# A macaron block's setup in one written order: loads, FFN weight, first tiles and the split of the other weights

## The chip, the cores and the metric

The kernel runs on one core of one Trainium2 chip. The metric is device time in microseconds (us), the median of three runs of the kernel before. Smaller is better.

## The reference

The input `x` has 4 x 4096 rows of 512 numbers. The block is: half an FFN, neighbourhood attention, half an FFN, each on a layer-normed input, with a residual.

```python
x = x + 0.5 * ffn(layernorm(x), weight, ffn_bias)
x = x + attention(layernorm(x), qkv_w, qkv_b, rpb, proj_w, proj_b)
x = x + 0.5 * ffn(layernorm(x), weight, ffn_bias)
```

The "FFN" is one 512 x 512 linear layer, `xd @ wd.T + bias`. Both its operands are first quantised in blocks of 32 along the row: the scale of a block is its largest magnitude over 7.5, the quotients are rounded to a grid of 6-bit floats, and multiplied by the scale again. The attention has 16 heads of 32; each of the 4096 rows of a sequence attends to 13 neighbours, with a relative bias table `rpb` of 16 x 25, and its output goes through the projection `proj_w`.

## The kernel before

**Tiles and products.** The 16384 rows are 128 tiles `t` of 128 rows. Four tiles are a group, and an attention item `m` is one group with one of four chunks of heads. Every 512-wide product is done in float16 with both operands split into a high and a low part: `product` (L139) issues 12 matmuls of 128 x 512. The weights lie transposed in one tile `wt` (L122), 20 chunks `o` of 128 output rows: 0 to 3 query, 4 to 7 key, 8 to 11 value, 12 to 15 projection, 16 to 19 FFN.

**The slots.** After the setup the order is a list of slots written out by hand. `begin(slot, stage)` puts a generator into a slot, `run_slot` runs its next part, and a part yields how many slots later its next one runs. One item takes `STEP` = 7 slots. A tile goes through `quantised_norms` (L213: factors on POOL, normalise on ACT, block maxima `sc` and reciprocals `r` on DVE, quotients `yq` on POOL, rounding `q` on ACT, scaling back `yq` on POOL, high part `hlq` on ACT, low part `hlq` on DVE, transposition to `xT` by a DMA from SP), `first_half` (L274: FFN product `pmf`, residual, statistics, normalise `yn`, high and low part `hln`, transposition into the group's tile `x2`), `values` (L296: product `pmv`, high and low part `vt`, a store of it to DRAM), and, from slot `QK` = 38 on, `project_qk` (L354: product `pmqk`, high part `qf` on ACT, low part on DVE), `softmax`, `attend`, `project_out` and `second_half`.

**The head.** It is what stands before slot `QK` (L673 to L891). It loads the FFN weight `fw`, three biases, the relative bias `rp`, the first tiles, and the 16 chunks `rows` of the other weights. Each weight matrix is scaled by a power of two, which `powers` (L716) makes from the largest sum of squares of a chunk: squares on ACT, a maximum `top` on DVE, a transposition `ptn` and a small product `pb` on TensorE, and eight small steps on DVE that give `up` and `down`. The FFN weight is quantised (L760 to L784), then split into high and low part and transposed by DMAs from SP. `put_scaled` (L795) does the split of the other chunks, through four buffers `whl`: ACT writes the high part, DVE the low part, and SP transposes it into `wt`. `attention_bias` (L827) adds the value bias's projection to `after_b`; `put_table` (L874) makes the table of relative biases from `shifted` (eight loads from the DRAM tile `rd`) and `masks` (four).

**What sets the order.** Up to L793 a scheduler in the language's library orders the instructions of each engine by its own estimate; from `tc.manual_schedule()` on they stand as the code issues them. Every engine then works through its own instructions in that order, and so does each queue of DMA issues: nearly all of them stand on SP, the loads of the two broadcast biases (L681, L682), of `b12` and of `rp` on ACT. A DMA from SP also waits until the DMA eight before it on the same set of semaphores has landed. The pools of the head are released at its end, and tiles of the attention reuse their memory.

Of the kernel before, what the change touches and what calls it, by code (L numbers as in the profile page):

```python
# [37 lines left out]
P = 128  # L38
# [25 lines left out]
def macaron_kernel(  # L64
# [148 lines left out]
    def quantised_norms(slot):  # L213
# [7 lines left out]
        if spare:  # L221
            y = xp.tile([P, dim], F32, tag="x", name=f"yq{slot}").unsqueeze(1)
        else:
            y = yp.tile([P, 2, dim], F32, tag="yq", bufs=2, name=f"yq{slot}")[:, :n]
# [16 lines left out]
        q8 = q8p.tile([P, 2, dim], F8, tag="q8", name=f"q8_{slot}")[:, :n]  # L241
# [6 lines left out]
        if spare:  # L248
# [355 lines left out]
    EARLY = 3  # L604
# [35 lines left out]

    for t in range(NT):
        k = t * STEP
        sooner = (0, 2, 5, STEP)[t] if t <= EARLY else 0
        begin(k - 18 - (STEP if t == EARLY else 0), one(load, t), 0)
        slot = k - 10 - (10 if t == EARLY else 0)
        enlist(slot, t, "n1")
        if not 0 < t < EARLY:
            begin(slot - 1, one(moments, slot, t, "n1"), 1)
        begin(k + F1 - sooner, first_half(t))
        begin(k + V, values(t))  # L650
        begin(k + F1 - sooner, one(add_bias, t, half_ffn_b), 8)
# [6 lines left out]
    for slot in together:  # L658
        if together[slot][0][0][1] == "n3" or together[slot][0][0][0] >= EARLY:
            begin(slot, quantised_norms(slot), 1)  # L660
# [11 lines left out]

    with tc.tile_pool(name="setup", bufs=1) as sp, tc.tile_pool(name="scratch", bufs=2) as scr:  # L673
# [4 lines left out]
        rp = sp.tile([HEADS, NREL + 2 * (QR - 1)], F32, name="rp")  # L678
        for o in range(KC):
            nc.sync.dma_start(out=fw[:, o, :], in_=ffn_w[o * P : (o + 1) * P, :])  # L680
        nc.scalar.dma_start(out=half_ffn_b, in_=ffn_b.partition_broadcast(P))  # L681
        nc.scalar.dma_start(out=after_b, in_=proj_b.partition_broadcast(P))  # L682
        nc.scalar.dma_start(out=b12, in_=qkv_b.rearrange("(c p) -> c p", p=P))
        nc.gpsimd.memset(rp, 0.0)
        nc.scalar.dma_start(out=rp[:, QR - 1 : QR - 1 + NREL], in_=rpb)


        rows = {}

        sq = sp.tile([P, 5 * KC], F32, name="sq")  # L690
        first = min(slots)
        for slot in range(first, first + EARLY * STEP, STEP):
            run_slot(slot)
        for _ in quantised_norms(-10):
            pass
        chunks = (8, 9, 10, 11, 12, 13, 14, 15, 0, 4, 1, 5, 2, 6, 3, 7)
        for o in chunks:
            w, i = (qkv_w, o) if o < 3 * KC else (proj_w, o - 3 * KC)
            rows[o] = xp.tile([P, dim], F32, tag="x", name=f"rows{o}")
            nc.sync.dma_start(out=rows[o], in_=w[i * P : (i + 1) * P, :])  # L700
        for o in (*range(4 * KC, 5 * KC), *chunks):
            src = fw[:, o - 4 * KC, :] if o >= 4 * KC else rows[o]
            junk = scr.tile([P, dim], BF16, tag="junk", name=f"junk{o}")
            nc.scalar.activation(junk, src, AF.Square, accum_out=sq[:, o : o + 1])
        ptb = ps_m.tile([P, 512], F32, tag="mm", name="ptb")
        nc.tensor.transpose(ptb[:, : 3 * KC], b12, ident[: 3 * KC, : 3 * KC])
        bT = sp.tile([P, 3 * KC], F32, name="bT")
        nc.vector.tensor_copy(bT, ptb[:, : 3 * KC])
        b2 = sp.tile([P, 3 * KC], F32, name="b2")
        nc.vector.scalar_tensor_tensor(b2, bT, 2.0 ** -8, bT, ALU.mult, ALU.mult)  # L710
        nc.vector.tensor_tensor(sq[:, : 3 * KC], sq[:, : 3 * KC], b2, ALU.add)
        top5 = sp.tile([P, 5], F32, name="top5")
        up = sp.tile([P, 5], F32, name="up")
        down = sp.tile([P, 5], F32, name="down")

        def powers(lo, hi):  # L716

            w = hi - lo
            nc.vector.tensor_reduce(
                top5[:, lo:hi], sq[:, lo * KC : hi * KC].rearrange("p (m c) -> p m c", c=KC),  # L720
                AX.X, ALU.max,
            )
            ptn = ps_m.tile([P, 512], F32, tag="mm", name=f"ptn{lo}")
            nc.tensor.transpose(ptn[:w, :P], top5[:, lo:hi], ident)
            most = sp.tile([w, 1], F32, name=f"most{lo}")
            nc.vector.tensor_reduce(most, ptn[:w, :P], AX.X, ALU.max)
            diag = sp.tile([w, w], F32, name=f"diag{lo}")
            nc.vector.tensor_scalar(diag, ident[:w, :w], most, 2.0, ALU.mult, ALU.mult)
            ones_w = sp.tile([w, P], F32, name=f"ones{lo}")
            nc.gpsimd.memset(ones_w, 1.0)  # L730
            pb = ps_m.tile([P, 512], F32, tag="mm", name=f"pb{lo}")
            nc.tensor.matmul(pb[:, :w], ones_w, diag, start=True, stop=True)
# [16 lines left out]
        def put_weights(o, hl):  # L749
# [3 lines left out]
            )  # L753

        w_sc, w_r, w_back = (
            sp.tile([P, KC * NB], F32, name=name) for name in ("w_sc", "w_r", "w_back")
        )
# [178 lines left out]
```

## Time and profile before

| | us |
|---|---|
| median of 3 runs (2294.38 to 2295.41) | 2294.65 |
| the profiled execution | 2295.28 |
| its span | 2293.5 |
| PE busy in the span | 2214.2 (97%) |
| DVE busy | 2011.7 (88%) |
| POOL busy | 1969.2 (86%) |
| ACT busy | 1695.5 (74%) |

PE is TensorE's matmuls, PEld its weight loads, DVE VectorE, ACT ScalarE, POOL GpSimd, SP SyncE; SPq is the queue of SP. A row of the timeline has the start in us from the span's start, the duration, the engine, the line, the operation, output and inputs, the shapes, the number of instructions merged into the row, and in brackets how long the engine had been idle and what it had waited for. The chain of waits is the work that ended last, followed back from the end, as start, duration and what it is. The time of any one run agrees with another of the same kernel within 0.05% here.

### The profile page before, as it was taken

What the parts mean: (1) busy time and instruction counts of PE and PEld (TensorE: products, weight loads), DVE (VectorE), ACT (ScalarE), POOL (GpSimd) and SP (SyncE); (2) the same over time, 40 slices, a digit from 0 to 9 for tenths busy, and PEclk for the clock granted to TensorE, in tenths of its full rate; (3) what the DMA queues carried; (4) which work ended last, traced back from release to release, by engine and by line L of the source; (5) the groups of instructions that cost most, each with busy time, mean ns of one, the idle gap of its engine ahead of it and who ended that gap; (6) DMA issues with size and microseconds to landing.
All of it is one profiled execution on the core that took longest, in us unless ns stands there. A gap on an engine that the chain in (4) does not pass through costs nothing.

```text
span 2293.5 us, 65425 instructions
## 1 busy us (share of the span) xinstructions
PE 2214.2 (97%) x26771; PEld 1052.9 (46%) x26771; DVE 2011.7 (88%) x3769; ACT 1695.5 (74%) x2544; POOL 1969.2 (86%) x2006
## 2 busy tenths in 40 slices
PE   3799999999999999999999999999999999999978
PEld 1344444444444444444444444444444444444433
DVE  6899998888988988898988998888988988989775
ACT  5697777777777777777777777777777777777752
POOL 4588988988988988888888888888888889888776
PEclk9999999999999999999999999999999999999989
DMA  7687776777767777777776776777776777866654
GB/s 201 153 178 161 162 160 154 159 162 158 160 156 155 164 162 154 161 158 157 162 158 155 162 161 154 160 157 155 164 160 151 167 158 154 166 155 147 137 107 104
DMA packets 926213, 359.61 MB, mean 157 GB/s; under 512 B 719452, under 2 KB 890328, under 8 KB 925912
## 3 DMA queue, kind: packets, MB, share of 16 engines
q1 hardware_dynamic: 925568, 354.90, 70.8%
q8 instruction: 209, 3.42, 0.6%
q14 instruction: 92, 0.75, 0.1%
q10 hardware_dynamic: 344, 0.53, 0.1%
HBM read 110.26 MB, written 67.29 MB: 77 GB/s over the span
## 4 chain that ended last, share of the span: by engine, by line
PE 87%; DVE 7%; ACT 2%; POOL 2%; DMA 1%; issue 1%; SPq 0%; ACTq 0%; DVEq 0%; POOLq 0%
PE pmqk L144 27%; PE pmf L144 26%; PE pmo L144 14%; PE pmv L144 13%; PE ps L458 4%; PE pv L549 3%; DVE stn L173 1%; DVE hlq L197 1%; DVE hln L197 1%; DVE sc L232 1%; ACT qk L390 0%; DVE x L272 0%; POOL yq L239 0%; DVE total L514 0%; DVE qf L383 0%
## 5 line engine op out<-in xcount | busy, mean ns | idle before, releaser
L144 PE MATMUL pmf<-wt,xT 128*128 128x512 f16 x3048 | 702.7, 381 | 13.3 <-DMA xT<-hlq 7.4
L144 PE MATMUL pmqk<-x,wt 128*128 128x512 f16 x3072 | 705.8, 379 | 0.4 <-DVE after_b L836 0.4
L144 PEld LDWEIGHTS <-xT 128*128 128x128 f16 x3048 | 298.4, 98 | 377.2 <-DMA xT<-hlq 15.2
L144 PEld LDWEIGHTS <-wt 128*128 128x128 f16 x3072 | 289.7, 98 | 336.0 <-issue 1.3
L239 POOL TENSOR_TENSOR yq<-yq,r 128x1024 f32<-128x1024 f32 (+1 forms) x141 | 247.1, 1752 | 135.6 <-DVE r L237 124.1
L144 PE MATMUL pmv<-wt,x 128*128 128x512 f16 x1536 | 353.9, 380 | 4.2 <-DVE qf L383 2.6
L144 PE MATMUL pmo<-wt,ring 128*128 128x512 f16 x1536 | 357.2, 383 | 0.0
L390 ACT ACTIVATE qk<-qf,parity 128x1024 f16<-128x1024 f16 x256 | 349.3, 1432 | 0.0
L610 POOL TENSOR_TENSOR x<-x,half_ffn_b 128x512 f32<-128x512 f32 x256 | 327.8, 1281 | 0.0
L272 DVE SCALAR_TENSOR_TENSOR x<-pmf,coef,x 128x512 f32<-128x512 f32 x256 | 180.0, 703 | 144.7 <-PE pmf L144 141.1
L576 ACT ACTIVATE ring<-pv 128x510 f16<-128x510 f32 (+7 forms) x176 | 78.7, 475 | 307.3 <-PE pv L549 234.4
L173 DVE BATCH_NORM_STATS2 stn<-x 128x6 f32<-128x512 f32 x384 | 265.2, 691 | 8.8 <-DMA x<-in_L_attn_x_dram 0.2
L244 POOL TENSOR_TENSOR yq<-q,sc 128x1024 f32<-128x1024 fp8e4 (+1 forms) x141 | 246.2, 1746 | 4.8 <-ACT q L242 4.8
L144 PEld LDWEIGHTS <-x 128*128 128x128 f16 x1536 | 150.5, 98 | 186.9 <-issue 4.9
L242 ACT ACTIVATE q<-yq,nudge 128x1024 fp8e4<-128x1024 f32 (+1 forms) x141 | 150.0, 1064 | 115.9 <-POOL yq L239 107.6
L144 PEld LDWEIGHTS <-ring 128*128 128x128 f16 x1536 | 141.2, 98 | 160.5 <-issue 5.0
L518 POOL TENSOR_TENSOR sf<-sf,total 128x714 f32<-128x714 f32 (+2 forms) x128 | 178.7, 1396 | 37.2 <-DVE total L516 19.3
L226 ACT ACTIVATE yq<-x,nbq,rsq 128x512 f32<-128x512 f32 x254 | 193.1, 803 | 16.7 <-POOL nbq L185 15.2
L525 POOL TENSOR_TENSOR p<-sf,p 128x714 f16<-128x714 f32 (+2 forms) x128 | 192.5, 1504 | 0.0
L509 POOL TENSOR_TENSOR sf<-sf,top 128x714 f32<-128x714 f32 (+2 forms) x128 | 182.4, 1425 | 3.5 <-DVE top L507 3.3
L197 DVE TENSOR_TENSOR hlq<-yq,hlq 128x1024 f16<-128x1024 f32 (+1 forms) x141 | 167.6, 1189 | 8.7 <-ACT hlq L193 6.6
L610 POOL TENSOR_TENSOR x<-x,after_b 128x512 f32<-128x512 f32 x128 | 162.9, 1274 | 0.0
(143 smaller groups left out, 3441.0 us busy)
## 6 DMA issues: line engine op xcount, KB each, us to landing
vs<-vd SPq DMA_DIRECT2D x144, 357.0 KB
x<-in_L_attn_x_dram SPq DMA_DIRECT2D x128, 256.0 KB
vd<-vt SPq DMA_DIRECT2D x128, 256.0 KB
out_dram<-x SPq DMA_DIRECT2D x128, 256.0 KB
vs<-vd SPq DMA_DIRECT2D x24, 378.0 KB
vs<-vd SPq DMA_DIRECT2D x24, 315.0 KB
rows<-in_L_attn_qkv_w_dram SPq DMA_DIRECT2D x12, 256.0 KB
xT<-hlq SPq DMA_TRANSPOSE x141
```

Of the source, the lines that this page charges most:

```text
L144: nc.tensor.matmul(pm, lhs(a, c), rhs(b, c), start=(n == 0), stop=(n == 3 * KC - 1))
L173: nc.vector.bn_stats(st, xs[t])
L197: nc.vector.tensor_tensor(hl[:, :, 1, :], y, hl[:, :, 0, :], ALU.subtract)
L226: nc.scalar.activation(y[:, u], xs[t], AF.Identity, bias=nb[:, u : u + 1], scale=rs[:, u : u + 1])
L239: nc.gpsimd.tensor_tensor(yb, yb, bc(r, QB), ALU.mult)
L244: nc.gpsimd.tensor_tensor(yb, q8.rearrange("p u (n q) -> p (u n) q", q=QB), bc(sc, QB), ALU.mult)
L272: nc.vector.scalar_tensor_tensor(xs[t], pm, cf, xs[t], ALU.mult, ALU.add)
L390: nc.scalar.activation(to, whole[0], AF.Copy, scale=parity[:, e : e + 1])
L509: nc.gpsimd.tensor_tensor(s, s, bc(top[:, :n], KN), ALU.subtract)
L518: nc.gpsimd.tensor_tensor(s, s, bc(total[:, :n], KN), ALU.mult)
L525: nc.gpsimd.tensor_tensor(p[:, :n, KN : 2 * KN], s, ph, ALU.subtract)
L610: nc.gpsimd.tensor_tensor(xs[t], xs[t], b, ALU.add)
```

## The change

The head is no longer ordered by the library's scheduler. `tc.manual_schedule()` is called ahead of it, every step becomes a small function, and each is entered in a list with a key. The list is sorted by the keys and run in that order; a key decides nothing but the place. What is computed is the same, but for the places where the arithmetic moves: the FFN weight's scale is applied in the split (`split`, as for the other chunks) and no longer in the factor `w_back`.

- Loads: `fw` in four pieces first, then `x` tiles 0 and 1, then the FFN bias row, then the query, key and value chunks with `x` tiles 2 to 4 between them. The four projection chunks, `x` tiles 5 and 6, the projection's bias row, `rp`, `masks` and `rd` come behind the FFN weight's transpositions. All but `b12` are issued by SP.
- The first seven tiles are normalised with buffers of their own (`own`), one tile at a time; `first_half` of tiles 0 to 4 and `values` of tiles 0 and 1 are in the list too. `values` of tile 2 and the product for the value bias are put into slots behind `QK`.
- The order of the chunks is 8 to 11, then query and key in pairs, and the projection's last.
- Two blocks of 12 matmuls into a tile that nobody reads (`idle`) follow the splits of the first and the last FFN chunk.

```diff
-    def quantised_norms(slot):
+    def quantised_norms(slot, own=None):
...
+        if own:
+            y = own.tile([P, 1, dim], F32, name=f"yq{slot}")
+        elif spare:
...
+        if own:
+            q8 = own.tile([P, 1, dim], F8, name=f"q8_{slot}")
+        else:
+            q8 = q8p.tile([P, 2, dim], F8, tag="q8", name=f"q8_{slot}")[:, :n]
...
+        if own:
+            hl = own.tile([P, 1, 2, dim], F16, name=f"hlq{slot}")
...
+    HEAD = 7
     for t in range(NT):
         k = t * STEP
-        sooner = (0, 2, 5, STEP)[t] if t <= EARLY else 0
-        begin(k - 18 - (STEP if t == EARLY else 0), one(load, t), 0)
-        slot = k - 10 - (10 if t == EARLY else 0)
-        enlist(slot, t, "n1")
-        if not 0 < t < EARLY:
+        if t >= HEAD:
+            if t > HEAD + 1:
+                begin(k - 18, one(load, t), 0)
+            slot = k - 10
+            enlist(slot, t, "n1")
             begin(slot - 1, one(moments, slot, t, "n1"), 1)
-        begin(k + F1 - sooner, first_half(t))
-        begin(k + V, values(t))
-        begin(k + F1 - sooner, one(add_bias, t, half_ffn_b), 8)
+        if k + F1 >= QK:
+            begin(k + F1, first_half(t))
+            begin(k + F1, one(add_bias, t, half_ffn_b), 8)
+        if k + V >= QK:
+            begin(k + V, values(t))
...
+    ctx.enter_context(tc.manual_schedule())
+    vbx = {}
     with tc.tile_pool(name="setup", bufs=1) as sp, tc.tile_pool(name="scratch", bufs=2) as scr:
...
-        for o in range(KC):
-            nc.sync.dma_start(out=fw[:, o, :], in_=ffn_w[o * P : (o + 1) * P, :])
-        nc.scalar.dma_start(out=half_ffn_b, in_=ffn_b.partition_broadcast(P))
-        nc.scalar.dma_start(out=after_b, in_=proj_b.partition_broadcast(P))
-        nc.scalar.dma_start(out=b12, in_=qkv_b.rearrange("(c p) -> c p", p=P))
...
+        ones = sp.tile([4, P], F32, name="ones")
+        nc.gpsimd.memset(ones, 1.0)
...
-        for slot in range(first, first + EARLY * STEP, STEP):
-            run_slot(slot)
-        for _ in quantised_norms(-10):
-            pass
...
+        def load_ffn(o):
+            rows[4 * KC + o] = fw[:, o, :]
+            nc.sync.dma_start(out=fw[:, o, :], in_=ffn_w[o * P : (o + 1) * P, :])
...
-        w_sc, w_r, w_back = (
-            sp.tile([P, KC * NB], F32, name=name) for name in ("w_sc", "w_r", "w_back")
-        )
...
-        nc.vector.tensor_scalar(w_back, w_sc, up[:, 4:5], None, ALU.mult)
-        for o in range(KC):
-            w8 = scr.tile([P, dim], F8, tag="w8_", bufs=KC, name=f"w8_{o}")
-            nc.scalar.activation(w8, fw[:, o, :], AF.Identity, bias=w_nudge, saturate=False)
-            nc.vector.tensor_tensor(blocks(fw[:, o, :]), blocks(w8), per(w_back, o), ALU.mult)
-            hl = scr.tile([P, 2, dim], F16, tag="whl", bufs=4, name=f"whlf{o}")
-            nc.scalar.copy(hl[:, 0, :], fw[:, o, :])
-            nc.vector.tensor_tensor(hl[:, 1, :], fw[:, o, :], hl[:, 0, :], ALU.subtract)
-            put_weights(4 * KC + o, hl)
-
...
+        def rounded(o):
+            w8[o] = scr.tile([P, dim], F8, tag="w8_", bufs=KC, name=f"w8_{o}")
+            nc.scalar.activation(w8[o], fw[:, o, :], AF.Identity, bias=w_nudge, saturate=False)
+
+        def scaled_back(o):
+            nc.vector.tensor_tensor(blocks(fw[:, o, :]), blocks(w8[o]), per(w_sc, o), ALU.mult)
+
+        def split(o):
             s = up[:, o // KC : o // KC + 1]
             hl = scr.tile([P, 2, dim], F16, tag="whl", bufs=4, name=f"whl{o}")
             nc.scalar.activation(hl[:, 0, :], rows[o], AF.Copy, scale=s)
-            yield 1, 9
+            yield
             nc.vector.scalar_tensor_tensor(
                 hl[:, 1, :], rows[o], s, hl[:, 0, :], ALU.mult, ALU.subtract
             )
-            put_weights(o, hl)
-
-        su, sd = up, down
+            nc.sync.dma_start_transpose(
+                out=wt.rearrange("p s c o -> p (s c) o")[:, :, o * P : (o + 1) * P],
+                in_=hl.rearrange("p s k -> p (s k)"),
+            )
+            if o in (4 * KC, 5 * KC - 1):
+                idle = ps_s.tile([P, 512], F32, tag="s", name=f"idle{o}")
+                for _ in range(12):
+                    nc.tensor.matmul(idle, hl[:, 1, :P], hl[:, 1, :], start=True, stop=True)
+
...
-        def attention_bias():
-
-            vbx = sp.tile([P, 2, KC, P], F16, name="vbx")
-            nc.scalar.copy(vbx[:, 0], bc(vb, P))
-            nc.vector.tensor_tensor(vbx[:, 1], bc(vb, P), vbx[:, 0], ALU.subtract)
-            yield 11, 9
-            pmb = ps_m.tile([P, dim], F32, tag="mm", name="pmb")
-            product(pmb, lambda s, c: vbx[:, s, c, :], lambda s, c: wt[:, s, c, PO : PO + dim])
-            yield 1, 9
-            nc.vector.scalar_tensor_tensor(after_b, pmb, cp, after_b, ALU.mult, ALU.add)
...
-        begin(0, one(scales), 9)
-        for slot, o in zip((2, 4, 5, 6, 10, 13, 16, 19, 21, 23, 25, 27, 29, 31, 33, 35), chunks):
-            begin(slot, put_scaled(o), 9)
-        begin(20, attention_bias(), 9)
-        begin(26, one(put_table), 9)
-        slot = first
-        while slot < QK:
-            run_slot(slot)
-            slot += 1
-
+        def attention_bias():
+            t = xp.tile([P, dim], F32, tag="x", name="vbx").bitcast(F16)
+            vbx[0] = t = t.rearrange("p (s c q) -> p s c q", s=2, c=KC)
+            nc.scalar.copy(t[:, 0], bc(vb, P))
+            yield
+            nc.vector.tensor_tensor(t[:, 1], bc(vb, P), t[:, 0], ALU.subtract)
+
+        order = []
+
+        def at(key, f, *args):
+            order.append((key, len(order), f, args))
+
+        def spread_out(gen, *keys):
+            for key in keys:
+                at(key, next, gen, None)
+
+        CHUNKS = (8, 9, 10, 11, 0, 4, 1, 5, 2, 6, 3, 7, 12, 13, 14, 15)
+        for o, key in enumerate((0.71, 1.13, 1.56, 1.99)):
+            at(key, load_ffn, o)
+        for t, key in enumerate((2.42, 2.87, 5.09, 7.07, 10.37, 26.1, 26.6) + (55.92, 61.92)):
+            at(key, load, t)
+        for o, key in zip(CHUNKS, (3.77, 4.43, 5.75, 6.41, 7.73, 8.39, 9.05, 9.71, 11.03, 11.69, 12.35, 13.01, 24.1, 24.6, 25.1, 25.6)):
+            at(key, load_row, o)
+        at(0.8, lambda: nc.scalar.dma_start(out=b12, in_=qkv_b.rearrange("(c p) -> c p", p=P)))
+        at(3.32, lambda: nc.sync.dma_start(out=half_ffn_b, in_=ffn_b.partition_broadcast(P)))
+        at(27.1, lambda: nc.sync.dma_start(out=after_b, in_=proj_b.partition_broadcast(P)))
+        at(27.6, lambda: nc.sync.dma_start(out=rp[:, QR - 1 : QR - 1 + NREL], in_=rpb))
+        at(5.97, lambda: nc.gpsimd.tensor_scalar(half_ffn_b, half_ffn_b, 0.5, None, ALU.mult))
+        for h, key in enumerate((28.1, 28.66, 29.22, 29.78)):
+            at(key, put_masks, h)
+        at(30.34, put_shifts)
+        for i, key in enumerate((32.34, 32.94, 33.54, 35.44, 36.04, 39.24, 39.84, 40.44)):
+            at(key, put_shifted, i // 4 * 2, i % 4)
+
+        for o in range(KC):
+            at((3.34, 4.02, 4.71, 5.6)[o], block_maxima, o)
+            at((3.33, 4.15, 4.97, 5.79)[o], square, 4 * KC + o)
+            at((8.89, 9.57, 12.87, 13.55)[o], quotients, o)
+            at((10.26, 10.96, 14.13, 14.84)[o], rounded, o)
+            at((14.23, 15.83, 17.26, 18.69)[o], scaled_back, o)
+            spread_out(split(4 * KC + o), (15.55, 16.98, 18.51, 19.84)[o], (16.53, 17.96, 19.39, 20.82)[o])
+        at(7.54, block_scales, 0)
+        at(7.99, block_scales, 2)
+        at(4.65, biases)
+        at(27.44, bias_squares)
+        spread_out(powers(4, 5), 7.19, 8.44, 10.25)
+        at(11.65, ffn_factor)
+        spread_out(powers(0, 4), 33.98, 37.57, 40.89)
+        at(49.26, scales)
+        for o, key in zip(CHUNKS, (6.63, 7.45, 8.61, 11.67, 12.49, 13.31, 20.55, 21.37, 22.19, 23.01, 23.83, 26.19, 28.45, 29.27, 30.81, 32.97)):
+            at(key, square, o)
+        for o, h, l in zip(CHUNKS, (42.75, 43.47, 44.19, 44.91, 47.08, 49.87, 50.59, 51.31, 52.03, 52.75, 53.47, 54.19, 55.73, 56.45, 57.77, 58.49), (44.74, 46.37, 47.1, 48.53, 51.46, 52.19, 53.62, 54.35, 55.08, 55.81, 56.54, 57.27, 59.85, 61.26, 62.81, 65.14)):
+            spread_out(split(o), h, l)
+        at(67.04, put_table)
+        spread_out(attention_bias(), 59.21, 69.29)
+
+        NORMS = (
+            (6.29, 7.47, 9.43, 11.7, 12.95, 16.26, 17.11, 19.22, 20.12),
+            (14.93, 15.91, 17.69, 21.55, 22.81, 24.65, 26.3, 27.83, 29.88),
+            (22.72, 23.9, 25.37, 26.27, 28.7, 30.09, 30.9, 32.35, 33.28),
+            (23.62, 25.11, 27.01, 27.91, 29.8, 31.63, 33.2, 35.24, 36.02),
+            (24.52, 35.6, 36.88, 38.92, 40.5, 42.03, 42.9, 49.25, 52.92),
+            (31.48, 36.8, 38.08, 58.68, 59.93, 61.11, 61.91, 63.09, 64.44),
+            (32.38, 45.22, 54.91, 65.87, 67.12, 68.3, 69.1, 70.41, 71.17),
+        )
+        for t, keys in enumerate(NORMS):
+            slot = t - 1000
+            enlist(slot, t, "n1")
+            at(keys[0], moments, slot, t, "n1")
+            spread_out(quantised_norms(slot, sp), *keys[1:])
+        FIRST = (
+            (25.8, 29.08, 30.58, 32, 33.79, 35.32),
+            (34.04, 36.77, 38.02, 39.3, 40.58, 42.34),
+            (37.14, 40.09, 43.04, 44.02, 45.63, 47.83),
+            (40.94, 43.94, 45.47, 46.45, 47.8, 50.76),
+            (59.29, 62.01, 63.54, 64.52, 65.8, 68.59),
+        )
+        for t, (keys, bias) in enumerate(zip(FIRST, (10.33, 18.59, 27.4, 34.3, 38))):
+            spread_out(first_half(t), *keys)
+            at(bias, add_bias, t, half_ffn_b)
+        for a, t, b in zip((54.08, 56.68), (0, 1), (57.17, 59.81)):
+            spread_out(values(t), a, b)
+        for _, _, f, args in sorted(order, key=lambda e: e[:2]):
+            f(*args)
+
+    def bias_product():
+        pmb = ps_m.tile([P, dim], F32, tag="mm", name="pmb")
+        t = vbx.pop(0)
+        product(pmb, lambda s, c: t[:, s, c, :], lambda s, c: wt[:, s, c, PO : PO + dim])
+        yield 1, 9
+        nc.vector.scalar_tensor_tensor(after_b, pmb, cp, after_b, ALU.mult, ALU.add)
+
+    begin(QK + 1, values(2), 6)
+    begin(QK + 9, bias_product(), 9)
+    slot = QK
 
```

`load_row`, `square`, `biases`, `bias_squares`, `block_maxima`, `block_scales`, `quotients`, `put_masks`, `put_shifts` and `put_shifted` hold the statements that stood in the head before, one step each; `powers` yields behind `ptn` and behind `pb`.

## Prediction

> **What bounds the kernel now.** I read busy time by stretches first.
>
> ```profile
> 0.00:82.40 82.40, 32.58 (x116) 13.16 (x117) 55.74 (x131) 46.33 (x92) 37.94 (x74) 0.94 0.75 188
> 82.40:105.00 22.60, 19.98 (x145) 8.78 (x145) 17.91 (x35) 15.79 (x24) 13.22 (x22) 0.92 0.55 133
> 105.00:200.00 95.00, 94.49 (x1316) 45.59 (x1315) 92.08 (x187) 85.01 (x132) 80.16 (x95) 1.00 0.78 174
> 200.00:300.00 100.00, 98.56 (x1256) 47.05 (x1255) 93.91 (x164) 77.52 (x121) 91.13 (x90) 1.00 0.74 160
> ```
>
> The columns are the stretch, its length, then PE, PEld, DVE, ACT, POOL. PE is solid behind 105 us, so a new head moves the end only by moving the moment from which PE runs solid. Next the timeline of PE, to find that moment.
>
> ```profile
> 35.47 0.37 PE L724 MATMUL ptn<-ident,top 128*4 128x128 f32 x1 [22.92 <-DVE top L719]
> ...
> 37.04 5.30 PE L144 MATMUL pmf<-wt,xT-10_170 128*128 128x512 f16 x12
> ...
> 87.73 2.75 PE L144 MATMUL pmf<-wt,xT 128*128 128x512 f16 x12
> 93.10 4.21 PE L144 MATMUL pmv<-wt,x 128*128 128x512 f16 x12 [2.62 <-DVE qf L383]
> 97.24 0.90 PE L458 MATMUL ps<-qk 64*64 64x84 f16 x64
> ...
> 239.58 2.75 PE L144 MATMUL pmf<-wt,xT 128*128 128x512 f16 x12 [1.44 <-DVE qf L383]
> ```
>
> It is 93.10. The first FFN product (37.04) stands behind ptn, which waits for the squares of all weights; that is far from the end of the head. The chain of waits says what holds 93.10:
>
> ```profile
> 28.70 2.81 DMA xT-10_170<-hlq-10_168
> ...
> 88.34 3.05 DMA wt<-whl
> 91.58 0.69 ACT qf L379
> 92.30 0.76 DVE qf L383
> 93.10 4.21 PE pmv L144 x12
> ```
>
> The first attention tile, qf, reuses memory of the setup pools, so it waits for the last transposition that reads them (issued 88.34, landed 91.39). I call this landing the gate. Last the queue of SP, which issues every transposition:
>
> ```profile
> 73.50 1.25 SPq L198 DMA_TRANSPOSE xT<-hlq  x1
> 74.85 1.26 SPq L198 DMA_TRANSPOSE x<-hln  x1
> 76.20 1.27 SPq L750 DMA_TRANSPOSE wt<-whl  x1
> 77.56 0.53 SPq L309 DMA_DIRECT2D vd<-vt  x1
> ```
>
> Back to back they start 1.35 us apart (73.50, 74.85, 76.20, 77.56), and land 2.8 to 3.05 after issue. Loads and stores take 0.65.
>
> **The change part by part.** The end moves by (new gate − 91.39) plus the PE work that moves behind the gate. I walk the new order with the rows' durations: ACT 0.62 to 0.72 for 128x512, 0.8 with a bias tile; DVE 0.66 to 0.74; a normalisation's three POOL factors together 1.3, its other POOL operations 1.05, a bias add 1.27.
>
> *Loads.* The two broadcast biases no longer run beside fw: the proj_b row goes to the far end, half_ffn_b behind x0 and x1. The lines of DVE and ACT give landings by the number of 256 KB pieces sent so far:
>
> ```profile
> 5.57 0.69 DVE L761 TENSOR_REDUCE w_sc<-fw 128x16 f32<-128x512 f32 x1 [4.66 <-DMA fw<-in_L_ffn_weight_dram]
> ...
> 10.62 0.69 DVE L173 BATCH_NORM_STATS2 stn<-x 128x6 f32<-128x512 f32 x1 [0.21 <-DMA x<-in_L_attn_x_dram]
> ```
>
> The third piece (fw0 and two biases) is there at 5.57, the eighth (x1) at 10.62, and the eleventh (rows8) at 12.84, where ACT starts on it. So the last fw is the fourth (6.8, before 8.5), x0 the fifth (7.9, before 9.4), and rows10 the eleventh (12.8). ACT squares rows10 ahead of tile 0's normalisation, which so ends at 14.3. DVE then has sc (1.1), two quotients (1.25), and scaled_back, moments and four lows to 23.95, paced by ACT. The last FFN transposition, fifth on SP from 20.05, is issued at 25.45 and lands at 28.4: the first FFN product starts there, 8.6 earlier. Gone are w_back (0.82) and a second memset of ones (0.19): no more, as ACT paces this part. The 24 added idle matmuls, 12 x 0.43 cold and 12 x 0.22 warm, run from 20.05 to 27.8, in PE's wait for that landing; without this cover, all cold, the first product starts at 30.4, 2 late, and x0's update with it.
>
> *The scales of the other weights come later.* SP now issues, behind the FFN transpositions: four proj rows, x5, x6, after_b and rp (8 x 0.45, to 30.4; three of these bias and table loads came from ACT's queue), four masks (0.6 each, each waiting for a proj row; behind whl19 the rows land at 29.2 to 31.3), tile 1's xT at 33.0, then rd at 34.3, whose landing the shifted loads wait for on SP. No row shows that landing: it lies between 0.7, rd's own issue, and 4.44, the loaded x that the chain of waits has at 6.16; I take 2.5, near the transpositions' 2.8, as the queue is short then. Behind that wait and two shifted loads of 0.65 is tile 2's xT: 38.2, landed 41.0. Behind it PE runs pmf 2 (2.75) and then pb, so the eight steps to `up` (0.2 each) end at 46.2. Before, up was there at 39.7. So the sixteen splits start 6.5 later, although the FFN stage is 8.6 earlier.
>
> *The last stretch.* Low 8 follows hln 1, statistics and x3 on DVE: SP issues it at 49.4. From there to tile 6's xT, the new last one, SP has 21 transpositions and four loads or stores: 21 x 1.35 + 4 x 0.65 = 31.0, which puts that issue at 80.4 if the queue never starves. It starves twice. The hln pieces share one buffer, and hln 2 is fourth from whl8 on SP: issued 53.5, landed 56.4, and only then ACT can write hln 3: 1.5 lost. And `whl` has four buffers: ACT's order is whl12, whl13, vt0, whl14, whl15, vbx, vt1. whl13 waits for the landing of whl6, the thirteenth (49.4 + 12 x 1.35 + 1.5, issued 67.2, landed 70.2); vt0's store stands before whl7 on SP; whl15 then waits for whl7's landing, and vt1's store, which stands before whl12 on SP, comes behind it: 70.2, vt0 71.6, low 72.2, whl7 issued 72.9, landed 75.8, whl15, vbx and vt1 copies 77.7, low 78.4. SP idles some 4 there. Then whl12, whl13, x8, whl14, xT 5, whl15, hln 4 take it to 88; and on the other engines tile 6's normalisation, queued on DVE behind low 15, does its POOL, ACT, POOL, ACT, DVE steps (1.1, 0.7, 1.05, 0.7, 0.7) just as late, to 88.5. The landing is 91.4. Means with both engines busy are longer than what I used (whl's low is 0.877 over 16, yq on POOL 1.165): half of that over the twelve or so such operations on the path is 1 us. Gate 92.4; bounds 82.5 (no starving, and hln 1 at 47.1 with whl8 next to it: 47.1 + 1.35 + 31.0 + 3.0) and 97 (the long rows of the third rival, and one more landing waited for).
>
> *Behind the gate.* pmf 5 ran ahead of it (87.73) and comes behind it now, with the bias product: 24 matmuls, 5.2 warm. PE's wait before is longer than 2.62, so those first 12 run cold, as the first product did: 5.30 where pmv took 4.21, at most +1.1, I take 0.7. Against that, idle time of PE that a later PE fills: 0.51 at 171 and 1.44 at 239.58, 0 to 1.95, I take 1.4. Sum: 92.4 − 91.4 + 5.2 + 0.7 − 1.4 = +5.5. The profiled execution spans 2293.5 and took 2295.28; the median, 2294.65, is 0.63 below that. 2294.65 + 5.5 = **2300**.
>
> The row behind 1.35 is SP's own: an issue is 1.25 long. The Trainium skill (DMA: Bandwidth & Descriptors, Latency and other measured facts) gives a DMA transpose 261 GB/s, or 350 to 400 where contiguous. By that, an estimate, a 256 KB transposition takes about 0.7 to 1.0, the queue of 21 is 7 to 13 shorter, and the change is faster. The trace shows no transposition closer than 1.35 to the next, so I keep the row.
>
> **The rivals.**
> - *SP's queue does not starve* (faster). Place: between hln 1 and tile 6's xT; price: 9 of the gate. Gate 82.5: −8.9 + 5.2 + 0.7 − 1.95 = −5, 2290; 1 less with the loads all at the 387 GB/s of the microsecond from 12. It decides once the gate is under 87. For it: SP has work of 1.35 each throughout; against it: the four buffers and vt1 behind whl15. 19 in 100.
> - *DVE bounds behind the gate.* The chain of waits runs over DVE from 111 to 239, DVE being 97% busy. Then PE's extra 5.9 is hidden and DVE's extra counts, vt2 and after_b (0.67 + 0.75): 1.0 + 1.4 = +2.4, 2297. Against: PE idles only 0.51 of 95. 16 in 100.
> - *Contention decides.* POOL has five normalisation products, three adds and six factor triples between 26 and 43; with the long rows (add 1.72, whl 1.5, factor 0.76 for 0.19) the scales come 3 to 4 later: gate 96, +9, 2304. 23 in 100.
> - My forecast: 42 in 100, its own range 2297 to 2303.
>
> **How the numbers follow.** 0.2% is 4.6, about what a measurement of this kernel can tell from no change. Slower by more: the third rival and two thirds of the forecast, 0.51. Within: the rest of the forecast, the DVE rival, and a quarter of the first, 0.35. Faster: 0.14. The range goes from the first rival's lower end to gate 97 with nothing filled (5.6 + 5.2 + 1.1): 2288 to 2307, less than 2 in 10 outside.
>
> **What would show it.** pmf of tile 0 starts near 28 (37.04 before). `up` for the four weights is ready near 46, the first whl transposition issued near 49. SP idles between whl7 and whl12, waiting for vt1's low. qf on ACT starts near 92 and waits for an xT landing, not for wt. PE's first product behind it is pmf 5, cold. I am wrong if whl transpositions start under 46, if ACT never waits for a whl landing, or if qf starts under 87.

## The result and the profile after

| | us |
|---|---|
| before, median of 4 runs (2293.19 to 2295.41) | 2294.52 |
| changed, median of 4 runs (2307.93 to 2309.71) | 2308.78 |
| the changed kernel's profiled execution | 2308.49 |
| its span (before 2293.5) | 2306.4 |

The ratio is 1.0063, with a 95% interval of 1.0045 to 1.0080: slower by 14.3 us. The prediction had 2300 and 2288 to 2307.

The first view is the busy time by stretches, with the columns of the prediction (stretch, length, PE, PEld, DVE, ACT, POOL, granted clock).

```profile
82.40:105.00 22.60, 10.95 (x38) 4.10 (x37) 13.96 (x25) 8.53 (x14) 9.26 (x12) 0.73 0.56 120
105.00:200.00 95.00, 95.00 (x1243) 45.47 (x1242) 88.45 (x183) 80.89 (x125) 73.94 (x90) 0.99 0.73 160
```

PE does not idle at all from 105 to 200, so again the end hangs on the moment from which PE runs solid. Between 82.4 and 105 it works 10.95 us where it had 19.98 before. The chain of waits (start, length, what) shows what it stands for.

```profile
94.03 1.05 POOL yq-994_713 L241
...
95.91 1.48 POOL yq-994_713 L249
97.41 0.63 ACT hlq-994_824 L193
...
98.06 0.70 DVE hlq-994_824 L197
...
98.82 3.04 DMA xT-994_826<-hlq-994_824
...
101.97 0.70 ACT qf L386
...
102.69 0.76 DVE qf L390
...
103.49 4.33 PE pmf L144 x12
```

The chain is the one foreseen: `qf` stands on the landing of tile 6's transposition (slot -994), and PE's first product behind it is tile 5's first FFN product. Only the hour is another, 101.86 for the landing in place of 92.4. How it came to be so late is first seen on SP.

```profile
39.69 0.65 SPq L851 DMA_DIRECT2D rd<-rp  x1
43.44 1.27 SPq L855 DMA_DIRECT2D shifted<-rd  x2
44.80 1.27 SPq L198 DMA_TRANSPOSE xT-998_491<-hlq-998_481  x1
...
56.35 4.18 SPq L814 DMA_TRANSPOSE wt<-whl  x3
...
81.04 0.39 SPq L316 DMA_DIRECT2D vd<-vt  x1
...
87.31 0.37 SPq L316 DMA_DIRECT2D vd<-vt  x1
```

The first split of the scaled weights leaves at 56.35 (before 42.62; predicted 49.4). ACT's waits from 50 to 104 (total, times, longest) name the second cause:

```profile
ACT whl L809 <- DMA wt<-whl: 13.4, 8, 4.3
```

Eight times ACT stands before a split until a transposition frees one of the four `whl` buffers. Before, ACT waited for none of them.

### The profile page after: what moved, and what is told of

Same layout as the page of the kernel before. It is cut to its first block, busy times and chain, and to the rows that moved or that the text cites. A ratio compares the mean times of both kernels' runs of the same rounds, so it can differ in the third digit from the quotient of the medians.

```text
span 2306.4 us, 65457 instructions
## 1 busy us (share of the span) xinstructions
PE 2220.4 (96%) x26795; PEld 1055.0 (46%) x26795; DVE 2025.3 (88%) x3770; ACT 1698.3 (74%) x2544; POOL 1973.0 (86%) x2005
## 4 chain that ended last, share of the span: by engine, by line
PE 90%; DVE 4%; DMA 2%; POOL 1%; ACT 1%; issue 1%; SPq 0%; DVEq 0%; ACTq 0%; POOLq 0%
PE pmqk L144 28%; PE pmf L144 27%; PE pmo L144 14%; PE pmv L144 13%; PE ps L465 4%; PE pv L556 3%; DMA wt<-whl 1%; DVE stn L173 1%; ACT qk L397 0%; DVE hlq L197 0%; DVE whl L811 0%; DVE x L279 0%; POOL yq L249 0%; DVE hln L197 0%; DMA xT<-hlq 0%
## 5 line engine op out<-in xcount | busy, mean ns | idle before, releaser
L144 PE MATMUL pmf<-wt,xT 128*128 128x512 f16 x2988 | 686.3, 380 | 7.1 <-DMA xT<-hlq 5.5
L144 PEld LDWEIGHTS <-xT 128*128 128x128 f16 x2988 | 292.2, 98 | 361.5 <-DMA xT<-hlq 7.4
L241 POOL TENSOR_TENSOR yq<-yq,r 128x1024 f32<-128x1024 f32 (+1 forms) x136 | 241.5, 1776 | 121.5 <-DVE r L239 106.4
L249 POOL TENSOR_TENSOR yq<-q,sc 128x1024 f32<-128x1024 fp8e4 (+1 forms) x136 | 241.3, 1774 | 1.9 <-ACT q L247 1.9
```

Of the source, the lines that this page charges most:

```text
L144: nc.tensor.matmul(pm, lhs(a, c), rhs(b, c), start=(n == 0), stop=(n == 3 * KC - 1))
L241: nc.gpsimd.tensor_tensor(yb, yb, bc(r, QB), ALU.mult)
L249: nc.gpsimd.tensor_tensor(yb, q8.rearrange("p u (n q) -> p (u n) q", q=QB), bc(sc, QB), ALU.mult)
```

## The experiments

All are edits of the changed kernel, but for `e10`. "Time" is the median; the changed kernel's own is 2308.78. The kernel before was measured again beside each: its medians were 2293.1 to 2293.9 (2294.52 beside the changed kernel), its single runs 2291.2 to 2295.7, which is wider than the 0.05% of its first three. So a difference to 2308.78 is good to some 1.5 us, and small ones are read from the traces.

### What the gate consists of

`e1_other_pool`: tiles 5 and 6 leave the setup pool.

```diff
-            spread_out(quantised_norms(slot, sp), *keys[1:])
+            spread_out(quantised_norms(slot, sp if t < 5 else None), *keys[1:])
```

> Edit: the normalisations of tiles 5 and 6 take their pieces from the pools of the steady loop, so the first attention tile qf shares memory with neither. In the changed kernel ACT's qf stood at 101.97, on the landing of tile 6's transposition (issued 98.82, landed 101.86). Theory (that landing is the gate and the end moves with it): now qf waits only for ACT's own hlq of tile 6 (97.41 to 98.03) and DVE's low of the bias tile (97.93), so it starts at 98.1, PE's first product behind it near 99.6, and the time falls by 3.9, to about 2304.9. Rival (DVE, not the gate, sets the end behind it): qf moves as much, but PE idles more before 240 and the time stays within 1 of 2308.8.

Measured: 2305.67, ratio to before 1.0056 (1.0041 to 1.0071), and `qf` no longer waits for a landing:

```profile
98.08 0.69 ACT L386 ACTIVATE qf<-pmqk,qk_b 128x512 f16<-128x512 f32 x1
```

3.9 off the gate, 3.1 off the median. The landing was the gate.

`e2_six_whl`: two more buffers.

```diff
-            hl = scr.tile([P, 2, dim], F16, tag="whl", bufs=4, name=f"whl{o}")
+            hl = scr.tile([P, 2, dim], F16, tag="whl", bufs=6, name=f"whl{o}")
```

> Edit: six buffers for the split weights where there were four. In the changed kernel ACT waits 13.4 us in 8 pieces for landings of whl transpositions between 53 and 85. Theory (this rotation starves SP's queue, and with it the gate): the order walked with six buffers loses about two of three of these waits, qf goes from 101.97 to about 96, and the time falls by 5 to 6, to about 2303. Rival (the waits are cover for other late work, tile 6's normalisation or the scales): qf moves under 2 and the time stays over 2306.5.

Measured: 2302.93, 1.0042 (1.0027 to 1.0057). ACT's waits for buffers and the gate of this kernel:

```profile
ACT whl L809 <- DMA wt<-whl: 5.3, 4, 2.8
```

```profile
95.23 0.69 ACT L386 ACTIVATE qf<-pmqk,qk_b 128x512 f16<-128x512 f32 x1 [3.94 <-DMA xT-994_826<-hlq-994_824]
```

8.1 of the 13.4 go, 6.7 of the gate, 5.9 of the time.

`e7_six_and_pool`: both edits.

> Edit: six whl buffers, and tiles 5 and 6 in the steady loop's pools, together. Alone they gave 2302.93 (-5.9) and 2305.67 (-3.1). Theory (rotation and tile 6's landing are separate pieces of one gate, and what is left against the kernel before is the 24 products, 5.2, that come behind it): the sum, -9 to -10, 2299 to 2300; qf near 92, as in the kernel before (91.58), and the time 5 to 6 over it. Rival (they are two names of one wait): no better than 2302.

Measured: 2299.22, 1.0025 (1.0015 to 1.0035). The two add up, 9.6 against 5.9 + 3.1. Against the kernel before of the same session the gains are 8.9, 4.5 and 1.7; one softmax product late in the steady loop begins 10.6, 6.1 and 3.6 earlier than in the changed kernel. Its PE, behind its gate:

```profile
92.43 4.41 PE L144 MATMUL pmf<-wt,xT-995_793 128*128 128x512 f16 x12 [6.94 <-DVE qf L390]
```

This is the row to keep. PE starts 0.67 earlier than before (93.10), and the time is 5.3 longer. What is left is work that stands behind the gate and stood ahead of it before.

### Whether the late scales hold the splits

`e3_shifts_late`: no transposition behind the wait for `rd`.

```diff
-        at(30.34, put_shifts)
-        for i, key in enumerate((32.34, 32.94, 33.54, 35.44, 36.04, 39.24, 39.84, 40.44)):
+        at(45.5, put_shifts)
+        for i, key in enumerate((60, 60.1, 60.2, 60.3, 60.4, 60.5, 60.6, 60.7)):
```

> Edit: rd is stored behind the first scaled weights and the eight shifted loads are issued far behind it, so that no transposition of tiles 2 and 3 stands on SP behind the wait for rd (39.69 to 43.43) and the first two shifted loads (1.3). Theory of the prediction (up is late because of this wait, and the gate follows up): tile 2's transposition is issued near 41 in place of 44.80, up is ready 3 to 4 earlier than 53.35, and the time falls by 3 to 4, to about 2305. Rival (the stretch behind up is bound by its own order; the eight loads moved into it cost SP 0.66 each): up is 2 to 4 earlier, but qf is not, it stays between 101 and 105, and the time is 2308 to 2312.

Measured: 2316.32, 1.0100 (1.0085 to 1.0115). Tile 2's transposition leaves 2.7 earlier (42.13), the step behind `up` ends 1.4 earlier (52.18), the first split leaves at 55.80. But the eight loads now stand among the splits:

```profile
90.36 5.19 SPq L855 DMA_DIRECT2D shifted<-rd  x8
...
103.10 1.25 SPq L198 DMA_TRANSPOSE xT-994_826<-hlq-994_824  x1
```

`qf` is at 106.34, 4.4 later, and PE's first products behind it take 5.28 and 3.00 where they had 4.33 and 2.75. Both sides missed: the rival had the direction, not the size.

`e6_scales_early`: all that the change put behind the FFN weight's transpositions goes back.

```diff
-        for o, key in zip(CHUNKS, (..., 13.01, 24.1, 24.6, 25.1, 25.6)):
+        for o, key in zip(CHUNKS, (..., 13.01, 13.1, 13.2, 13.3, 13.4)):
...
-        for h, key in enumerate((28.1, 28.66, 29.22, 29.78)):
+        for h, key in enumerate((13.6, 13.61, 13.62, 13.63)):
...
-        at(30.34, put_shifts)
+        at(13.05, put_shifts)
...
-        spread_out(powers(0, 4), 33.98, 37.57, 40.89)
+        spread_out(powers(0, 4), 28.4, 28.9, 29.0)
...
```

> Edit: projection's rows, the table's row, rd, masks and shifted loads go back to SP ahead of the FFN weight's transpositions, and the squares of projection's rows, and the three steps to up, ahead of tile 0's update: this undoes the named part of the change. The splits, the norms and the rest keep their order. Theory of the prediction (up is late, and the gate follows up): up is ready near 40 as in the kernel before (39.70; 53.35 in the changed one), the gate is 7 to 13 earlier, and the time 2296 to 2302. Rival (the scales are not what the splits wait for: ACT reaches the first split at 53.35 behind the norms and halves written ahead of it, having waited 1.39 for up): up is near 40, the first whl transposition still issued after 54, qf within 2 of 101.97, and the time 2307 to 2311.

Measured: 2315.17, 1.0089 (1.0072 to 1.0106). The scales are ready at 44.74, 8.9 earlier, and the first split leaves at 60.84, 4.5 later. It isn't clean: the shifted loads (21.73 to 27.08) hold the FFN weight's second and later transpositions on SP, so the first FFN product starts at 36.72 in place of 31.84, and `qf` stands at 106.04, where neither side had it. Hence the next one.

`e11_rows_early_alone`: the rows, their squares and the three steps alone; masks, `rd` and the shifted loads stay.

> Edit on the changed kernel: projection's rows are issued on SP behind the other rows (SP stood idle from 15.0 to 20.6), their squares on ACT and the three steps to up ahead of tile 0's update; masks, rd and the shifted loads stay where the change put them, so that the FFN weight's transpositions are not held as in the run with all of them moved (27.18 in place of 20.59). Theory of the prediction (the gate follows up): up near 40 in place of 53.35 and the gate 7 to 13 earlier, 2296 to 2302. Rival (the splits stand on ACT and DVE behind the first halves written ahead of them, and wait for the order): up near 40, the first whl transposition still at 56 to 59, the gate 0 to 3 later, for the squares stand ahead of the norms now: 2308 to 2313.

Measured: 2312.89, 1.0087 (1.0072 to 1.0103). On DVE, SP and ACT:

```profile
38.91 0.16 DVE L768 TENSOR_SCALAR down<-e 128x4 int32<-128x4 int32 x1
```

```profile
58.43 4.17 SPq L814 DMA_TRANSPOSE wt<-whl  x3
```

```profile
103.37 0.69 ACT L386 ACTIVATE qf<-pmqk,qk_b 128x512 f16<-128x512 f32 x1 [3.93 <-DMA xT-994_826<-hlq-994_824]
```

The scales are there 14 us earlier (the same step ended at 53.39), the FFN weight's transpositions leave as in the changed kernel (20.58), and the first split still leaves 2 later: the rival's case. What stands ahead of its low part on DVE:

```profile
56.99 0.75 DVE L279 SCALAR_TENSOR_TENSOR x<-pmf,coef,x 128x512 f32<-128x512 f32 x1 [1.88 <-PE pmf L144]
57.66 0.74 DVE L811 SCALAR_TENSOR_TENSOR whl<-rows,up,whl 128x512 f16<-128x512 f32 x1
```

It is written behind tile 3's residual, which waits for that tile's FFN product. Here the scales do not hold the splits; the order written ahead of them does. In the changed kernel itself ACT waits 1.39 for `up` ahead of its first split, at 53.35.

### What that order costs on DVE

`e5_factors_on_dve`: 19 operations of the head go from POOL to DVE.

```diff
-        nc.gpsimd.tensor_tensor(yb, yb, bc(r, QB), ALU.mult)
+        (nc.vector if own else nc.gpsimd).tensor_tensor(yb, yb, bc(r, QB), ALU.mult)
...
-            at(bias, add_bias, t, half_ffn_b)
+            at(bias, lambda t=t: nc.vector.tensor_tensor(xs[t], xs[t], half_ffn_b, ALU.add))
```

> Edit: the 14 multiplications (yq by r, q by sc) and the five bias additions of the head run on DVE where they ran on POOL, in the same places of the order; what is computed is the same. In the changed kernel DVE operations on two operands of SBUF end about one lone duration after a POOL operation that runs when they start: low of whl18 1.74 from 23.37 (POOL 23.30 to 24.56; alone 0.74), hlq of tile 1 1.46 from 36.86 (POOL 36.73 to 37.78; alone 0.68), and POOL's factors likewise (0.54, 0.94, 0.80 for 0.19, 0.55, 0.27 at 19.41). Theory (the two run one after the other, so 19 operations of 1.05 to 1.27 on POOL cost DVE's chain more than 19 of 0.69 on DVE itself): the long rows go, up is ready 2 to 3 earlier (53.35 before), qf 2 to 3 earlier, the time falls by 2 to 3, to about 2306.5. Rival (POOL's work runs beside DVE's, the long rows are chance): DVE has 19 x 0.61 = 11.6 more in its queue, on the chain that holds the gate; qf and the time are 2 to 4 later, 2311 to 2313.

Measured: 2311.57, 1.0073 (1.0058 to 1.0088). First the changed kernel's rows on DVE and POOL:

```profile
36.86 1.46 DVE L197 TENSOR_TENSOR hlq-999_438<-yq-999_324,hlq-999_438 128x512 f16<-128x512 f32 x1
...
40.65 1.32 DVE L197 TENSOR_TENSOR hlq-998_481<-yq-998_402,hlq-998_481 128x512 f16<-128x512 f32 x1
...
41.98 1.67 DVE L197 TENSOR_TENSOR hln<-yn,hln 128x512 f16<-128x512 f32 x1
```

```profile
36.73 1.05 POOL L249 TENSOR_TENSOR yq-998_402<-q_-998_459,sc-998_423 128x512 f32<-128x512 fp8e4 x1
...
40.38 1.05 POOL L249 TENSOR_TENSOR yq-997_431<-q_-997_473,sc-997_440 128x512 f32<-128x512 fp8e4 x1
41.38 1.71 POOL L616 TENSOR_TENSOR x<-x,half_ffn_b 128x512 f32<-128x512 f32 x1
```

POOL's operation of 36.73 ends at 37.78, and DVE's ends at 38.32, 0.54 behind; 41.43 and 41.97; 43.09 and 43.65. Each time DVE ends 0.54 to 0.56 behind POOL, little less than one lone duration (0.68). The same three rows of `e5`, without POOL's operations:

```profile
36.63 0.69 DVE L197 TENSOR_TENSOR hlq-999_438<-yq-999_324,hlq-999_438 128x512 f16<-128x512 f32 x1
...
40.96 0.68 DVE L197 TENSOR_TENSOR hlq-998_481<-yq-998_402,hlq-998_481 128x512 f16<-128x512 f32 x1
...
42.24 0.68 DVE L197 TENSOR_TENSOR hln<-yn,hln 128x512 f16<-128x512 f32 x1
```

So the exclusion is shown by the rows, and the expected gain did not come: the first split leaves at 57.14, `qf` stands at 102.59, the time is where the rival had it, though POOL's work does not run beside DVE's as the rival said. Why it did not come is read from the busy time of one stretch, first of the kernel before, then of the changed one, then of `e5`:

```profile
14.20:56.30 42.10, 15.58 (x50) 6.23 (x51) 27.78 (x72) 27.43 (x59) 18.96 (x26) 0.96 0.72 179
```

```profile
14.20:56.30 42.10, 22.15 (x75) 8.17 (x75) 35.33 (x69) 28.31 (x57) 27.59 (x39) 0.88 0.59 154
```

```profile
14.20:56.30 42.10, 22.01 (x75) 8.21 (x75) 35.51 (x83) 28.23 (x57) 11.19 (x23) 0.88 0.59 156
```

In this stretch, which ends at the changed kernel's first split, DVE (the third number behind the length) is busy 66% in the kernel before and 84% in the changed one. In `e5` POOL falls by 16 us and DVE by nothing: ten long rows, 7.7 us over their lone durations, went, and 14 more operations of some 0.6 came. So DVE ends its step `top`, for which PE waits, only 0.3 earlier (41.72 for 42.05). That was lost again on PE, whose next product, tile 1's, ran slower; these are its rows in the changed kernel and in `e5`:

```profile
42.27 4.25 PE L144 MATMUL pmf<-wt,xT-999_456 128*128 128x512 f16 x12
```

```profile
41.95 5.32 PE L144 MATMUL pmf<-wt,xT-999_456 128*128 128x512 f16 x12
```

It ends 0.75 later, and the split leaves 0.8 later. What the exclusion alone costs the gate, this run does not measure.

### What stands behind the gate

`e4_two_ahead`: tile 5's first product and the bias product are issued to PE before the slots.

```diff
+        at(71.2, next, ahead[0], None)
+        at(71.3, bias_product)
...
-    begin(QK + 9, bias_product(), 9)
+    begin(QK + 1, bias_sum(), 9)
+    begin(QK + 3, ahead[0], 8)
```

> Edit: tile 5's first FFN product and the bias product are issued to PE ahead of the gate, in its idle 10.6 us before 103.49; what follows them stays in the steady loop. Theory (PE is solid behind the gate, so each product put behind it costs its 2.6): the landing of tile 5's transposition (95.8) lets the first run from 95.9 to about 100.5, the bias tile's low (97.9) the second, cold or not, to 103 to 105; the time falls by 3.5 to 5.2, to 2303.6 to 2305.3. Rival (DVE bounds behind the gate, the 24 products were hidden): the time stays within 1 of 2308.8.

Measured: 2311.26, 1.0079 (1.0063 to 1.0096): a miss of both. ACT says why.

```profile
106.60 0.69 ACT L386 ACTIVATE qf<-pmqk,qk_b 128x512 f16<-128x512 f32 x1 [8.26 <-PE pmqk L144]
```

In PE's queue the two came ahead of the two products that `qf` and `qk` read (81.07 and 87.34 in the changed kernel, 103.80 here), and pushed these and another 12 matmuls behind the gate: 24 matmuls were exchanged for 36.

`e10_bias_behind`, on the kernel before: the bias product alone goes to its later slot.

```diff
...
-            yield 11, 9
+            yield QK + 9 - 20, 9
```

> Edit on the kernel before, alone: the bias product's 12 matmuls (and the sum into after_b) leave the head and run at the slot where the changed kernel has them, behind the gate; vbx stands in the pool of x. Theory (PE is solid behind the gate, a product put behind it costs its 2.6, less at most 1.95 of idle time that it fills): 2294.5 + 0.7 to 2.8, 2295.2 to 2297.3, and by half of the idle time 2296.2. Rival (DVE bounds behind the gate, the product is hidden): 2294.5 within 0.7, or lower, as DVE's and PE's work in the head is less.

Measured: 2295.47, ratio 1.0008 (0.9999 to 1.0018), +1.7 in the medians. It falls into the theory's range, but the interval does not part it from nothing. The traces say more. Below is the start of one softmax product, the third from the end, which shows where the steady loop stands (one profiled execution of each kernel; `e12` is one of the three kernels of the next part).

| | products put behind `qf` | `qf` | against before | softmax product | against before |
|---|---|---|---|---|---|
| before | | 91.58 | | 2185.91 | |
| `e10` | 1 | 90.45 | -1.1 | 2187.54 | +1.6 |
| `e7` | 2 | 90.17 | -1.4 | 2190.95 | +5.0 |
| changed | 2 | 101.97 | +10.4 | 2201.53 | +15.6 |
| `e12` | 0 | 81.44 | -10.1 | 2176.66 | -9.3 |

With one product put behind `qf` the loop falls back by 2.8 against it. With both it falls back by 5.2 to 7.4 (the changed kernel, `e1`, `e2`, `e3`, `e5`, `e6`, `e7`, `e11`; in `e4` `qf` waits for PE itself). With none it falls back by 0.9 to 1.6. So the products are not hidden, and what is left in `e7` is mainly their price.

### A version that beats both

`e8_relaid_eight`, `e9_relaid_six`, `e12_relaid_again`: the edits of `e7` (with eight buffers in `e8`, six in the others), tile 5's first product and the bias product in the list with their sums, and a new place for every step of the head.

```diff
-        for _, _, f, args in sorted(order, key=lambda e: e[:2]):
+        for _, _, f, args in sorted(((k, n, f, a) for k, (_, n, f, a) in zip([...], order)), key=lambda e: e[:2]):
```

> Edit on the changed kernel: eight whl buffers, tiles 5 and 6 in the steady loop's pools, tile 5's first product and the bias product (with their DVE steps) in the head ahead of qf, and the written order's keys laid anew: each engine's queue was walked with the durations of the rows, POOL's and DVE's operations on two SBUF operands one after the other, and steps were moved where the walk put an engine in wait. Theory (the order, not the work, holds the gate at 91 to 102): gate near 80, 11 to 13 ahead of the kernel before, nothing put behind it, so 2282 to 2285. Rival (SP's 32 transpositions and the loads that share its queue are near their limit at 91, or DVE's 90% share behind the gate hides the gain): 2290 or more.

> The same as the relaid kernel with eight buffers, with six, and another walk of the keys. Theory: the rotation costs little once the splits are spread; gate near 79, 2281 to 2284. Rival: six buffers starve SP again, 2 or more over the kernel with eight.

> A further walk of the keys of the relaid kernel with six buffers, which took 2287.09 with qf at 82.93 where its walk had 77.3. Theory: 1 to 2 less again, 2285 to 2287. Rival: the walk is too coarse for steps of this size, 2287 to 2290.

| | us | ratio to before | `qf` |
|---|---|---|---|
| `e8` | 2292.71 | 0.9995 (0.9985 to 1.0004) | 87.78 |
| `e9` | 2287.09 | 0.9972 (0.9963 to 0.9982) | 82.93 |
| `e12` | 2284.79 | 0.9963 (0.9951 to 0.9976) | 81.44 |

`e8` missed its range: one transposition of a second norm waits 6.5 on SP for DVE, and `qf` for PE. `e9` missed its own by 3. The lead over `e9` that `e8`'s two more buffers should give did not show, but the places of the steps differ as well. `e12` beats both kernels. Its SP, its ACT's waits and its PE:

```profile
45.02 1.28 SPq L815 DMA_TRANSPOSE wt<-whl  x1
...
48.37 1.23 SPq L815 DMA_TRANSPOSE wt<-whl  x1
...
51.70 2.62 SPq L815 DMA_TRANSPOSE wt<-whl  x2
```

```profile
ACT whl L810 <- DMA wt<-whl: 3.9, 2, 2.0
```

```profile
82.33 5.34 PE L144 MATMUL pmv<-wt,x 128*128 128x512 f16 x24
88.43 0.74 PE L465 MATMUL ps<-qk 64*64 64x84 f16 x64 [0.76 <-DVE r L239]
```

The splits start 11 earlier and come singly or in pairs between the other transpositions (the changed kernel issues up to four in a row), and PE is solid from 77.14 to 105 but for 0.76. What each of the moved steps gives was not tried.

## Why the prediction was wrong

**Right.** The mechanism: the end moves with the gate, the gate is tile 6's landing, pmf 5 is first behind it, and the two products come on top. SP's standing for both `vt` stores is there too (6.1 us in two pieces). The rival in which SP does not starve, and the one in which DVE hides PE's extra, fell: the first by ACT's 13.4, the second by PE's 95.00 of 95.

**Wrong: the size of the gate.** "Gate 92.4; bounds 82.5 ... and 97": it was 101.86, out of its own bounds. The sum had two parts.

- The first split at 49.4 was 56.35: 7.0 of the 9.5. The lag grows along the prediction's own chain: the first FFN product 3.4 (31.84 for 28.4), tile 1's transposition 5.3 (38.35 for 33.0), tile 2's 6.6 (44.80 for 38.2), `up` 7.1 (53.3 for 46.2). The chain of waits of the changed kernel passes through these:

```profile
27.84 3.75 DMA wt<-whl
31.84 4.33 PE pmf L144 x12
...
36.95 1.37 DVE hlq-999_438 L197
...
39.69 3.73 DMA rd<-rp
...
44.80 2.77 DMA xT-998_491<-hlq-998_481
...
53.15 0.17 DVE up L767
```

The first product took 4.33 (2.75 when warm), the low part behind it is one of the long rows, and the wait for `rd` was 1.2 longer than chosen. The prediction let the splits follow "the scales of the other weights come later". They came later, but `e11` gives them back 14 us and the split leaves no earlier: the tiles' first halves, written ahead of it on DVE, hold it too. What I did not do was to add up DVE's own queue up to that split: it is busy 35.3 of 42.1 us. I took lone durations (0.66 to 0.74) and gave "1 us" for "means with both engines busy"; the ten long rows alone hold 7.7. That without these the split would leave 7 earlier was not shown: `e5` removed them at the price of as much new work. Nor is the sum alone the cause: in the same stretch DVE is busy 33.2 in `e11`, which splits 2 later, and 34.1 in `e12`, which splits 11 earlier. The place of the steps in the queue decides.
- From there to the landing 43.0 was 45.5. "It starves twice" was one wait of ACT for the buffer of `hln` (2.9, foreseen as 1.5) and eight for a `whl` buffer (13.4 in all; foreseen were two). `e2` puts 5.9 on two more buffers, `e1` 3.1 on tile 6's place, `e7` 9.6 on both.

The third rival ("contention decides", 96, 2304) named the long rows and gave them 3 to 4. It was nearest in kind, and still half of the size.

A page bears on this which the prediction should have weighed. The Trainium skill (SBUF — State Buffer, SBUF: two separate sides) says that VectorE and GpSimd share one pair of ports, that a VectorE operation with two SBUF inputs competes for it with a GpSimd operation that reads SBUF, and that the one that starts first holds it until it ends, "an exclusive lock, not a bandwidth split". This case agrees: 1.46, 1.32 and 1.67 where 0.68 is the lone duration.

There was also a fault of method. I walked the new order with lone durations and subtracted the measured gate of the old one (91.39), in which all such waits are contained. Walked the same way, the two orders should have erred on the same side, and the difference should have lost some of the error; this was not tried. A walk is coarse in any case: that of `e9` had `qf` at 77.3, where it stood at 82.93.

**Behind the gate** I had +5.2, +0.7 for a cold start, -1.4 for idle time filled: +4.5. The steady loop runs 15.6 later (the softmax product begins at 2185.91 before and at 2201.53 after), 10.39 of it from PE's restart (93.10 to 103.49), so the terms came to 5.2, about the 24 warm matmuls alone. The cold start cost 0.12 more than before (4.33 against 4.21), and next to nothing was filled: up to 256 there are gaps of 0.22 and 1.60 in place of 0.51 and 1.44. At the end of the span 12.9 of the 15.6 are left; the last section says where most of the 2.7 went.

**The small steps.** The first FFN product started at 31.84, not 28.4: the last FFN transposition was issued at 27.84 (25.45) and took 3.75 to land. `rd` took 3.73 to land where I had chosen 2.5 between 0.7 and 4.44. The idle matmuls stayed under their cover.

## What to carry to other kernels

In a head where several engines hand small steps to each other, add up each engine's queue to the point in question, with the durations that its rows have beside the other engines, before following dependencies; then walk the old and the new order in the same manner and take only the difference. A burst of splits needs as many buffers as it is long, or steps between them: look for waits of the writer on the reader's landing. Memory that a setup shares with the loop makes the setup's last transfer a gate, and what the gate holds up is worth placing ahead of it.

## What was not expected of the hardware

The tail, which the change does not touch, gave 2.7 of the 15.6 us back. These are two of its rows before, then after:

```profile
2202.31 5.10 PE L144 MATMUL pmo<-wt,ring 128*128 128x512 f16 x12
...
2235.93 15.72 PE L144 MATMUL pmf<-wt,xT 128*128 128x512 f16 x60
```

```profile
2217.96 3.54 PE L144 MATMUL pmo<-wt,ring 128*128 128x512 f16 x12
...
2249.74 14.81 PE L144 MATMUL pmf<-wt,xT 128*128 128x512 f16 x60
```

The same 12 matmuls behind the same idle 4.09 took 5.10 in one kernel and 3.54 in the other (2.75 when warm), the 60 took 15.72 and 14.81: together 2.47. In the other kernels the 12 take 3.6 to 5.2. The granted clock over the 12 was 0.53 before and 0.77 after, over the 60 it was 0.83 and 0.88; what decides it no run here shows. A change of the head alone can so move the end by some 2 us more or less than the loop moved.

Two single rows beside this. An operation on DVE that reads PSUM and one SBUF operand did not wait for POOL: the update of `x` took 0.75 at 46.56 beside a POOL addition of 46.26 to 47.53. A very small operation did wait: a step of `powers` on 128x4 integers took 1.03 at 52.09 where its neighbours took 0.17, beside a POOL multiplication of 52.04 to 53.09.
